# Recurrent block on one core: first gated q^T of a sequence one slot ahead, results kept in traced order on SP, one token sum on another engine

## The chip, the cores and the metric

The kernel runs on one core of a Trainium2 chip. The metric is device time in microseconds of one execution. The engines are named as in the profile: PE (TensorE) multiplies matrices, DVE (VectorE), ACT (ScalarE) and POOL (GpSimd) work on elements, and SP (SyncE) issues most of the transfers between DRAM and SBUF.

## The reference

Eight sequences of 1024 tokens, 512 values each, in fp32. What is computed, cut to what matters:

```python
xn = layernorm(x)                                   # 8 x 1024 x 512
q, gate = xn @ Wq, softmax(xn @ Wg)                 # D = 128, three gates
for i in range(3):                                  # three decays
    k, v = xn @ Wk[i], xn @ Wv[i]
    w = sigmoid(decay_logits[i]) ** max(t - s - 1, 0) * (t > s)
    blended += gate[i] * (((q k^T) * w) v)
s = blended @ Wo * out_scale
g = silu(ffn(xn))        # ffn: silu(xn Gate^T) * (xn Up^T), then Down^T; INTER = 1376
out = x + s * g          # Gate, Up, Down = lut[idx], a table of 16 values
```

## The kernel before

**Two phases.** `phase_1` (0 to 675 us of the profile) makes normalized and transposed tokens, the recurrent part and the weights of the ffn, and leaves all of them in DRAM. `phase_2` (675 to 2227 us) is the ffn and the output. The change touches `phase_1` alone.

**Phase 1, by sequence.** `tokens` loads x in blocks of 128 tokens (SP, L345), takes statistics (DVE for the first two sequences, ACT for the others; POOL raises the variance to the power -0.5), normalizes (DVE, L379, for sequences 0 and 1; ACT, L381 and L382, for the rest), transposes on PE (`pt`, L391) and copies to SBUF on ACT (L392). Values, keys and queries come from `plain` for sequence 0, and from `nodes` for sequences 1 to 7. `nodes` forms its products after Strassen's manner (a block product in seven smaller ones) and needs four sums of the token blocks: `sums_of_tokens` makes t1 (L473) and t2 (L474) on DVE, t3 (L475) and t4 (L476) on POOL; t2 needs t1, and t4 needs t2. `softmax` makes the gates; they are turned around through DRAM: a write of 4-byte elements (L452) and reads that broadcast them over 128 partitions (L457). `keep_tokens` writes the tokens and their sums to DRAM for phase 2 (L480 to L483).

**The recurrence.** `chunks(b)` goes through the 8 chunks of a sequence from the last to the first. For each: `gated(c)` multiplies the gates into q^T (`ga`, L649, POOL; DVE for the last sequence) and that with a table (`qb`, L653, POOL; not for the first chunk taken); PE forms scores (`psc`, L674), DVE weighs them with the decay (`pr`, L676), PE adds up the state (`pu`, L682) and the result (`po`, L696), ACT copies it out (`bl`, L698), SP writes it (L699). Work on a chunk is cut in three parts by `yield`. `gated` is called one chunk ahead, but the first one of a sequence stands at the head of `chunks`.

**The ffn's weights.** `ffn_weights` is a generator of small steps. For each panel of 128 rows it loads indices from 0 to 15, looks them up (`look_up`, DVE, L200, L203, L207, L224), forms sums (POOL, L253 to L279) and writes the panel to DRAM (SP: `quadd`, `wgud`, `wdd`). Panels live in `wgu` with two buffers.

**Order.** Everything of phase 1 is interleaved by hand. The prologue has 12 slots (`plain`), then follow 8 slots for every sequence b, in which `chunks(b-1)` and `nodes(b)` run side by side. A slot has three parts; each begins with `tick()`, which counts down what `defer(parts, issue)` has put off, and pulls some steps of the generators: `fresh` (tokens), `weights`, `older` (chunks) and `newer` (nodes). `sums_of_tokens(b+1)` is called in the last part of the last slot. `keep_order` pins the order so traced for PE, DVE, ACT and POOL; SP is pinned only until slot 3 of the prologue. From there the framework's scheduler may let one SP transfer pass another.

Of the kernel before, what the change touches and what calls it, by code (L numbers as in the profile page):

```python
# [20 lines left out]


ENGINES = (mybir.EngineType.PE, mybir.EngineType.DVE, mybir.EngineType.Activation, mybir.EngineType.Pool)


def keep_order(tc, seen, engines=ENGINES):
# [11 lines left out]
def recurrent_block(ctx: ExitStack, tc, x, wq, wk, wv, wo, wg, decay_logits, out_scale, lut, gidx, uidx, didx, out):  # L38
# [73 lines left out]


    later = []

    def defer(parts, issue):
        later.append([parts, issue])
# [111 lines left out]
    def ffn_weights(build, pool, pair_pool):  # L229
# [9 lines left out]
        def gate_up(o):  # L239
            s, m = OCH[o]  # L240
            n = 2 * NV * m
            idx = build.tile([P, NB], I32, name="idx", tag="idx", bufs=2)
            iv = idx[:, :n].rearrange("p (a b) -> p a b", b=m)
            gs, us = (src[:, s : s + m].rearrange("(c p) b -> p c b", p=P) for src in (gidx, uidx))
            nc.sync.dma_start(out=iv[:, 2:6, :], in_=gs)
            nc.sync.dma_start(out=iv[:, 0:2, :], in_=us[:, 0:2, :])
            nc.sync.dma_start(out=iv[:, 6:8, :], in_=us[:, 2:4, :])
            yield
            wf = pool.tile([P, 2 * NB], F32, name="wgu", tag="wgu", bufs=2)
            yield from look_up(build, wf[:, :n], idx[:, :n], P, n)  # L250
            w = wf[:, : 2 * n].rearrange("p (k two m) -> p k two m", two=2, m=m)
            a21, a11, a12, a22, s1, s2, s3, s4 = (w[:, k] for k in range(8))
            nc.gpsimd.tensor_tensor(s1, a21, a22, ALU.add)  # L253
            nc.gpsimd.tensor_tensor(s2, s1, a11, ALU.subtract)
            yield
            nc.gpsimd.tensor_tensor(s3, a11, a21, ALU.subtract)
            nc.gpsimd.tensor_tensor(s4, a12, s2, ALU.subtract)
            wide = wf[:, 2 * m : 2 * n].rearrange("p (a b) -> p a b", b=m)
            if o >= 4 * NQ:
                defer(3, lambda: nc.sync.dma_start(out=wgu_d[o], in_=wide))  # L260
            if o >= 2 * NK:
                return
            to = quad_d[o // 4][:, :, o // 2 % 2, :].rearrange("p k (t m) -> p k t m", m=P)
            if o % 2 == 0:
                upper.append(w[:, 1:])
                defer(3, lambda: nc.sync.dma_start(out=to[:, :, 0:2, :], in_=w[:, 1:]))
                return
            up, low = upper.pop(), w[:, 1:]
            b21, b22, b11, b12 = low[:, :, 0], low[:, :, 1], up[:, :, 0], up[:, :, 1]
            pair = pair_pool.tile([P, 7, P], F32, name="pair", tag="pair")  # L270
            nc.gpsimd.tensor_tensor(pair, b11, b21, ALU.subtract)
            if o >= 4 * NQ:
                for _ in range(6):
                    yield
            nc.gpsimd.tensor_tensor(b21, b21, b22, ALU.add)
            yield
            nc.gpsimd.tensor_tensor(b11, b21, b11, ALU.subtract)
            yield
            nc.gpsimd.tensor_tensor(b12, b12, b11, ALU.subtract)  # L279
            defer(2, lambda: nc.sync.dma_start(out=to[:, :, 4:6, :], in_=up))  # L280
            defer(3, lambda: nc.sync.dma_start(out=to[:, :, 2:4, :], in_=low))
            defer(3, lambda: nc.sync.dma_start(out=to[:, :, 6, :], in_=pair))
            for _ in range(3):
                yield

        def down_tail():
            s, m = OCH[-1]
            idx = build.tile([P, NB], I32, name="idx", tag="idx", bufs=2)
            nc.sync.dma_start(out=idx[:m, :V], in_=didx[s : s + m, :])
            yield  # L290
            wf = pool.tile([P, 2 * NB], F32, name="wgu", tag="wgu", bufs=2)
            yield from look_up(build, wf[:m, :V], idx[:m, :V], m, V)
            defer(2, lambda: nc.sync.dma_start(out=wdt_d, in_=wf[:m, :V]))

        def down(j):
            idx = build.tile([P, NB], I32, name="idx", tag="idx", bufs=2)
            for a in range(2):
                nc.sync.dma_start(out=idx[:, ts(a, V)], in_=didx[ts(j + a * NK, P), :])
            yield
            t = pool.tile([P, 2 * NB], F32, name="wgu", tag="wgu", bufs=2)  # L300
            yield from look_up(build, t[:, : 2 * V], idx, P, 2 * V)
            b11, b12, b21, b22, t1, t2, t4 = (t[:, ts(k, V // 2)] for k in range(7))
            nc.gpsimd.tensor_tensor(t1, b12, b11, ALU.subtract)
            nc.gpsimd.tensor_tensor(t2, b22, t1, ALU.subtract)
            yield
            nc.gpsimd.tensor_tensor(b12, b22, b12, ALU.subtract)
            nc.gpsimd.tensor_tensor(t4, b21, t2, ALU.subtract)
            defer(3, lambda: nc.sync.dma_start(out=wd_d[j], in_=t[:, : 7 * V // 2]))

        jobs = [gate_up(o) for o in range(NO)] + [down_tail()] + [down(j) for j in range(NK)]  # L310
        next(jobs[0])
# [19 lines left out]
    xnTs = {}  # L331

    def tokens(xp, xnp):

# [37 lines left out]
        def normalize(s):  # L374
            if s >= B * NC:
                return
            xt, (m, r, h) = xts[s], scalars(s)
            if s < 2 * NC:
                nc.vector.tensor_scalar(xt, xt, m, r, ALU.add, ALU.mult)  # L379
            else:  # L380
                nc.scalar.mul(h, m, r)  # L381
                nc.scalar.activation(xt, xt, AF.Identity, bias=h, scale=r)  # L382
# [51 lines left out]
    def softmax(att, b, v_sb, gates, hf, n, waits):  # L434
# [14 lines left out]

        def write():  # L450
            with nc.allow_non_contiguous_dma(reason="1536 words or 3072"):
                nc.sync.dma_start(out=there.rearrange("k p -> p k"), in_=g.rearrange("p c i -> p (c i)"))  # L452

        def read(half):
            m = NC // NHALF * NI
            gates[half] = att.tile([P, m, P], F32, name=f"ga{b}_{half}", tag="ga")
            nc.sync.dma_start(out=gates[half], in_=gT_d[b][ts(half, m), :].partition_broadcast(P))  # L457

        defer(2, write)
        for half, parts in waits:  # L460
            defer(parts, lambda half=half: read(half))

# [5 lines left out]
    def sums_of_tokens(tp, b):  # L468
# [3 lines left out]
        t1, t2, t3, t4 = (ts_[:, k] for k in range(4))  # L472
        nc.vector.tensor_tensor(t1, b12, b11, ALU.subtract)  # L473
        nc.vector.tensor_tensor(t2, b22, t1, ALU.subtract)  # L474
        nc.gpsimd.tensor_tensor(t3, b22, b12, ALU.subtract)  # L475
        nc.gpsimd.tensor_tensor(t4, b21, t2, ALU.subtract)  # L476

    def keep_tokens(b):
        xnT, ts_ = xnTs[b], tss[b]
        nc.sync.dma_start(out=xs_d[b][:, 0:4, :], in_=xnT[:, :, :U])  # L480
        nc.sync.dma_start(out=xs_d[b][:, 4:6, :], in_=xnT[:, 2:4, U:])
        for k in (0, 2):
            nc.sync.dma_start(  # L483
                out=xs_d[b][:, 6 + 2 * k : 10 + 2 * k, :], in_=ts_[:, k : k + 2].rearrange("p a b u -> p (a b) u")
            )

    def plain(sides, att, kept):
# [25 lines left out]
        for k in range(NC + NC // 2):  # L513
            half = iter(())
            if k == NC // 2:
                values(NC - k)
                half = softmax(att, 0, v_sb, gates, 1, NC // NHALF, [(1, 6)])
            if NC // 2 <= k < NC:
                features(1, k - NC // 2, next_role())
            if k >= NC:  # L520

                features(0, k - NC, ("pa", "pe", "pb", "pc")[k - NC])
            if k == NC:
                half = softmax(att, 0, v_sb, gates, 0, NC // NHALF, [(0, 6)])
            next(half, None)
            yield
            next(half, None)
# [107 lines left out]

    def chunks(b, pools, kept):

        chk, blp = pools
        v_sb, gates, qT, kT = kept.pop(b)
        pu = p_r.tile([P, NI, P], F32, name=f"pu{b}", tag="r")  # L640
# [13 lines left out]
            return qa, qb  # L654

        following = gated(NC - 1)
        for c in reversed(range(NC)):
            last = c == NC - 1
            first = c == 0
# [36 lines left out]
                nc.tensor.matmul(po, lhsT=lh, rhs=rh, start=(n == 0), stop=(n == len(prods) - 1))  # L696
            bl = blp.tile([P, P], F32, name=f"bl{b}_{c}", tag="bl")
            nc.scalar.copy(bl, po)  # L698
            defer(1, lambda bl=bl, c=c: nc.sync.dma_start(out=bl_d[b][:, ts(c, P)], in_=bl))  # L699
            if not first:  # L700
                new = chk.tile([P, NI, P], F32, name=f"R{b}_{c}", tag="R")
                if last or not at_end:
# [11 lines left out]
    def phase_1():  # L714
        nonlocal small, p_a, p_c, p_r
        with (
# [8 lines left out]
            tc.tile_pool(name="wgup", bufs=1) as wgup,  # L725
            tc.tile_pool(name="att", bufs=2) as att,
            tc.tile_pool(name="chk", bufs=2) as chk,
            tc.tile_pool(name="blp", bufs=2) as blp,
            tc.tile_pool(name="pairp", bufs=1) as pairp,
            tc.tile_pool(name="small", bufs=3) as small,  # L730
        ):
# [22 lines left out]
            sums = sums_of_weights(sides)  # L754
            for k in range(NC + NC // 2):

                two = k == NC - 1 or k > NC
                tick()
                some(fresh, 3)
                next(setup, None)  # L760
# [3 lines left out]
                next(more, None)  # L764
                tick()
                next(first)
                some(weights, k >= NC // 2)
                some(fresh, 3 * two)
                some(weights, 2 * (k >= NC // 2))
                tick()  # L770
                next(first)
                if k == NC:
                    keep_tokens(0)
                if k >= NC:
                    next(sums)
                if k == 3:
                    keep_order(tc, seen, (mybir.EngineType.SP,))
            sums_of_tokens(tp, 1)
            for b in range(1, B + 1):
                older = chunks(b - 1, (chk, blp), kept)  # L780
                newer = nodes(b, sides, att, kept) if b < B else iter(())
                for k in range(NC):
                    tick()
# [11 lines left out]
                    tick()  # L795
                    next(fresh, None)
                    next(older, None)
                    if k == NC - 1 and b + 1 < B:
                        sums_of_tokens(tp, b + 1)
                    some(weights, 2 * (b < B))  # L800
                    some(newer, 1 - k % 2)
                for g in (older, newer):
                    for _ in g:
# [2 lines left out]
                pass  # L806
            while later:
                tick()

# [482 lines left out]
```

## Time and profile before

| | us |
|---|---|
| median of 3 runs (2225.44, 2225.83, 2227.60) | 2225.83 |
| the profiled execution | 2228.99 |
| its span | 2227.2 |
| phase 1 in it, to the first work of phase 2 | 675 |
| PE busy, DVE, ACT, POOL | 2135.3, 1196.0, 868.7, 1088.1 |
| mean granted clock of PE | 0.982 |

Busy times are sums over an engine's instructions within the span. The granted clock is the share of full speed that PE was allowed. Of a wait the profile names the engine that waited, and after an arrow what released it. Boundaries between sequences, taken as the end of the last product of `nodes` (`pcq`, L621) ahead of `sums_of_tokens`, lie at 98.85 (the end of the prologue), 167.75, 249.72, 331.40, 414.90, 489.98 and 565.70 us.

### The profile page before, as it was taken

To read this page: it belongs to the slowest core of one execution; us is meant where nothing else is said; L and a number is where in the kernel's file an instruction comes from. 1 tells how busy PE (TensorE), PEld (TensorE's weight loads), DVE (VectorE), ACT (ScalarE), POOL (GpSimd) and SP (SyncE) were. 2 spreads that over 40 slices of the span, in tenths; PEclk is the share of its full clock that TensorE was granted. 3 is DMA by queue.
4 is the path that set the end of the run, shared out by engine and by line. 5 is a ranking of instruction groups with operands and counts; after the bars stand their busy time and mean duration, and the time that the engine had idled before them with its cause. 6 is when DMAs were issued, how large, how long until landed. Compare 5 with 4: busy or idle time off the path is not lost.

```text
span 2227.2 us, 27197 instructions
## 1 busy us (share of the span) xinstructions
PE 2135.3 (96%) x9766; PEld 1698.1 (76%) x9766; DVE 1196.0 (54%) x1690; ACT 868.7 (39%) x1901; POOL 1088.1 (49%) x975
## 2 busy tenths in 40 slices
PE   9598897999889999999999999999999999999998
PEld 5477666768766878877887887788788778778877
DVE  7688686668862543543454355345335434534543
ACT  2376565667333422431441243144124314413520
POOL 2767646646433535455453454545344554634442
PEclk9799998999999999999999999999999999999999
DMA  7664454652354433442443344244334424434421
GB/s 185 185 149 150 153 158 154 187 165 73 125 195 160 161 120 123 156 161 87 147 147 116 130 157 159 83 151 147 115 136 151 151 97 152 143 113 144 151 72 52
DMA packets 158460, 309.55 MB, mean 139 GB/s; under 512 B 51731, under 2 KB 94230, under 8 KB 156278
## 3 DMA queue, kind: packets, MB, share of 16 engines
q1 hardware_dynamic: 148486, 283.16, 40.0%
q0 software_dynamic: 7728, 23.86, 2.9%
q8 instruction: 77, 1.26, 0.3%
q10 hardware_dynamic: 2112, 0.79, 0.1%
q14 instruction: 57, 0.47, 0.1%
HBM read 233.98 MB, written 73.80 MB: 138 GB/s over the span
## 4 chain that ended last, share of the span: by engine, by line
PE 88%; POOL 4%; DVE 4%; DMA 2%; issue 1%; ACT 1%; SPq 0%; POOLq 0%; DVEq 0%; ACTq 0%
PE s L918 31%; PE ds L1157 22%; PE sE L918 5%; PE fs L868 4%; PE po L696 3%; PE ds L1168 2%; PE ps L1179 2%; PE pcq L621 2%; PE paq L621 2%; PE peq L621 2%; PE psc L674 2%; PE fsE L868 2%; PE pu L682 1%; PE pev L600 1%; DVE leaf L207 1%
## 5 line engine op out<-in xcount | busy, mean ns | idle before, releaser
L918 PE MATMUL s<-xs,wq 128*128 128x256 f32 x3192 | 715.1, 379 | 0.0
L918 PEld LDWEIGHTS s<-xs,wq 128*128 128x128 f32 x3192 | 605.7, 190 | 94.0 <-issue 7.4
L1157 PE MATMUL ds<-wd,s 128*128 128x256 f32 x1280 | 286.7, 379 | 0.0
L1157 PEld LDWEIGHTS ds<-wd,s 128*128 128x128 f32 x1280 | 243.2, 190 | 33.1
L1157 PE MATMUL ds<-wd,h 128*128 128x256 f32 x960 | 222.9, 379 | 0.0
L1157 PEld LDWEIGHTS ds<-wd,h 128*128 128x128 f32 x960 | 182.3, 190 | 52.5 <-issue 27.1
L1012 POOL TENSOR_TENSOR u<-u,e 128x512 f32<-128x512 f32 x64 | 79.9, 1271 | 276.0 <-DVE u L1008 276.0
L941 DVE TENSOR_TENSOR s<-s,e 128x512 f32<-128x512 f32 x133 | 93.0, 700 | 202.8 <-ACT s L940 202.8
L1182 POOL TENSOR_TENSOR gx<-gx 128x512 f32<-128x512 f32 x63 | 80.3, 1274 | 184.3 <-DVE gx L1180 183.6
L945 DVE TENSOR_TENSOR sE<-s,e 128x512 f32<-128x512 f32 x133 | 93.0, 699 | 102.5 <-PE s L918 102.5
L918 PE MATMUL sE<-xs,wq 128*128 128x256 f32 x532 | 136.5, 379 | 0.0
L936 ACT COPY e<-sE 128x512 f32<-128x512 f32 x133 | 77.9, 586 | 136.5 <-PE sE L918 136.3
L852 POOL TENSOR_TENSOR xs<-xs 128x1792 f32<-128x1792 f32 (+1 forms) x38 | 127.8, 3382 | 1.0
L1198 ACT ACTIVATE gx<-ds 128x256 f32<-128x256 f32 x32 | 12.3, 385 | 285.9 <-PE ds L1168 285.9
L207 DVE TENSOR_SCALAR leaf<-idx,lut_x,lut_sb 128x1024 int32<-128x1024 int32 (+2 forms) x119 | 113.7, 983 | 0.0
L940 ACT COPY s<-s 128x512 f32<-128x512 f32 x133 | 75.8, 570 | 96.8 <-PE s L918 96.8
L929 ACT COPY s<-s 128x512 f32<-128x512 f32 x133 | 75.8, 570 | 95.2 <-PE s L918 92.7
L918 PEld LDWEIGHTS sE<-xs,wq 128*128 128x128 f32 x532 | 101.1, 190 | 13.7
L1190 DVE TENSOR_TENSOR pw<-ds,pw 128x256 f32<-128x256 f32 x32 | 13.6, 425 | 177.0 <-PE ds L1157 177.0
L1016 POOL TENSOR_TENSOR h<-h,e 128x512 f32<-128x512 f32 x64 | 80.0, 1274 | 57.5 <-issue 46.4
L674 PE MATMUL psc<-ga,kT 128*128 128x128 f32 x384 | 58.8, 293 | 51.0 <-POOL ga L649 50.6
L674 PEld LDWEIGHTS psc<-ga,kT 128*128 128x128 f32 x384 | 54.8, 204 | 67.6 <-POOL ga L649 53.9
(220 smaller groups left out, 3799.3 us busy)
## 6 DMA issues: line engine op xcount, KB each, us to landing
wq<-quadd SPq DMA_DIRECT2D x112, 896.0 KB, 4.5
xs<-xsd SPq DMA_DIRECT2D x8, 3584.0 KB, 11.8
wq<-quadd SPq DMA_DIRECT2D x42, 448.0 KB, 4.0
x<-in_x SPq DMA_DIRECT2D x64, 256.0 KB, 4.9
xsd<-ts SPq DMA_DIRECT2D x16, 1024.0 KB, 4.1
gx<-in_x SPq DMA_DIRECT2D x64, 256.0 KB, 2.8
out<-gx POOLq DMA_DIRECT2D x63, 256.0 KB, 2.3
quadd<-wgu SPq DMA_DIRECT2D x15, 896.0 KB, 4.7
```

The source lines that it names most:

```text
L207: nc.vector.tensor_scalar(o.bitcast(I32), iv, lut_x[:rows, k, :], lut_i[:rows, k, 0:1], ALU.bitwise_and, ALU.bitwise_xor,)
L621: nc.tensor.matmul(ps, lhsT=wq_k[k][:, v, ts(n, D)], rhs=xk[k][:, v, :], start=start and v == 0, stop=False, skip_group_check=True,)
L674: nc.tensor.matmul(psc[:, i, :], lhsT=kc[:, i, :], rhs=qa[:, i, :], start=True, stop=True)
L852: nc.gpsimd.tensor_tensor(o, x1, x2, ALU.subtract)
L868: nc.tensor.matmul(ps, lhsT=w[:, 2 * W_OF[k] + n, :m], rhs=xs[:, X_OF[k], 2 * n : 2 * n + 2, :], start=start and n == 0, stop=stop and n == 1,
L918: nc.tensor.matmul(self.t[n][:, ts(a, H)], lhsT=self.w[:, a, (0, 1, 5, 3, 2, 4, 6)[i - 1], :], rhs=self.xs[:, X_OF[self.ks[a]], D_OF[i], : ...
L941: nc.vector.tensor_tensor(self.t[1], self.t[1], self.e, ALU.add)
L945: nc.vector.tensor_tensor(self.t[3], self.t[2], self.e, ALU.add)
L1012: nc.gpsimd.tensor_tensor(o[:, n], o[:, n], other[:, n], ALU.add)
L1016: nc.gpsimd.tensor_tensor(of_h(half, n), of_h(half, n), two(other[:, n]), ALU.mult)
L1157: nc.tensor.matmul(ps, lhsT=lhs[k][:, n, :], rhs=wd_sb[n][:, ts(D_OF[k], H)], start=start and n == 0, stop=stop and n == NK - 1, skip_grou ...
L1182: (nc.vector if end else nc.gpsimd).tensor_tensor(g, g, xr, ALU.add)
```

## The change

- The first `gated` of a sequence is issued one slot ahead: `chunks` yields right after it, and `phase_1` makes and starts `chunks(b)` in the last slot of the sequence before, ahead of `sums_of_tokens(b + 1)`.
- t3 goes from POOL to DVE.
- Transfers of results (weights, gates, tokens, `bl`) and the reads of the gates are issued by `put`, and `keep_behind` gives each of them an order behind the SP instruction traced ahead of it. Transfers that are no results (x, indices) stay free.
- Sequence 1's tokens: ACT normalizes them (`s < NC` where it was `s < 2 * NC`), and the prologue takes double steps of `fresh` at slots 5, 7, 9 and 11, where they were at 7, 9, 10 and 11.
- The write of the gates is put off by 1 part (was 2); sequence 0's reads by 8 and 10 (were 6 and 6).
- The write of `bl` is put off by 2 parts (was 1), and `bl` has four buffers (were two).
- The last four slots of the prologue take no weight steps beyond the first pull of each slot (three fewer for each), and each later slot takes seven (was six). After an odd panel `ffn_weights` yields eight times (was three).
- `keep_tokens(0)` is split over slots 8 and 9.

The diff, cut to its lines:

```diff
 ENGINES = (mybir.EngineType.PE, mybir.EngineType.DVE, mybir.EngineType.Activation, mybir.EngineType.Pool)
+def keep_behind(tc, seen, names):
+    last = None
+    order = mybir.DependencyInfo(mybir.DependencyClass.NoSync, mybir.DependencyReason.DATA)
+    for i in tc.nc.cur_bb.bb.instructions:
+        if i.name not in seen and i.engine == mybir.EngineType.SP:
+            if last and i.name in names:
+                tc.add_manual_dep(i, last, order, reason="behind what was traced before")
+            last = i.name
...
     later = []
+    behind = set()
+    def put(out, in_):
+        nc.sync.dma_start(out=out, in_=in_)
+        behind.add(nc.cur_bb.bb.instructions[-1].name)
...
             if o >= 4 * NQ:
-                defer(3, lambda: nc.sync.dma_start(out=wgu_d[o], in_=wide))
+                defer(3, lambda: put(out=wgu_d[o], in_=wide))
             if o >= 2 * NK:
                 upper.append(w[:, 1:])
-                defer(3, lambda: nc.sync.dma_start(out=to[:, :, 0:2, :], in_=w[:, 1:]))
+                defer(3, lambda: put(out=to[:, :, 0:2, :], in_=w[:, 1:]))
                 return
...
             nc.gpsimd.tensor_tensor(b12, b12, b11, ALU.subtract)
-            defer(2, lambda: nc.sync.dma_start(out=to[:, :, 4:6, :], in_=up))
-            defer(3, lambda: nc.sync.dma_start(out=to[:, :, 2:4, :], in_=low))
-            defer(3, lambda: nc.sync.dma_start(out=to[:, :, 6, :], in_=pair))
-            for _ in range(3):
+            defer(2, lambda: put(out=to[:, :, 4:6, :], in_=up))
+            defer(3, lambda: put(out=to[:, :, 2:4, :], in_=low))
+            defer(3, lambda: put(out=to[:, :, 6, :], in_=pair))
+            for _ in range(8):
                 yield
...
             yield from look_up(build, wf[:m, :V], idx[:m, :V], m, V)
-            defer(2, lambda: nc.sync.dma_start(out=wdt_d, in_=wf[:m, :V]))
+            defer(2, lambda: put(out=wdt_d, in_=wf[:m, :V]))
...
             nc.gpsimd.tensor_tensor(t4, b21, t2, ALU.subtract)
-            defer(3, lambda: nc.sync.dma_start(out=wd_d[j], in_=t[:, : 7 * V // 2]))
+            defer(3, lambda: put(out=wd_d[j], in_=t[:, : 7 * V // 2]))
...
             xt, (m, r, h) = xts[s], scalars(s)
-            if s < 2 * NC:
+            if s < NC:
                 nc.vector.tensor_scalar(xt, xt, m, r, ALU.add, ALU.mult)
...
             with nc.allow_non_contiguous_dma(reason="1536 words or 3072"):
-                nc.sync.dma_start(out=there.rearrange("k p -> p k"), in_=g.rearrange("p c i -> p (c i)"))
+                put(out=there.rearrange("k p -> p k"), in_=g.rearrange("p c i -> p (c i)"))
             gates[half] = att.tile([P, m, P], F32, name=f"ga{b}_{half}", tag="ga")
-            nc.sync.dma_start(out=gates[half], in_=gT_d[b][ts(half, m), :].partition_broadcast(P))
-
-        defer(2, write)
+            put(out=gates[half], in_=gT_d[b][ts(half, m), :].partition_broadcast(P))
+        defer(1, write)
         for half, parts in waits:
...
         nc.vector.tensor_tensor(t2, b22, t1, ALU.subtract)
-        nc.gpsimd.tensor_tensor(t3, b22, b12, ALU.subtract)
+        nc.vector.tensor_tensor(t3, b22, b12, ALU.subtract)
         nc.gpsimd.tensor_tensor(t4, b21, t2, ALU.subtract)
-    def keep_tokens(b):
+    def keep_tokens(b, parts=(0, 1)):
         xnT, ts_ = xnTs[b], tss[b]
-        nc.sync.dma_start(out=xs_d[b][:, 0:4, :], in_=xnT[:, :, :U])
-        nc.sync.dma_start(out=xs_d[b][:, 4:6, :], in_=xnT[:, 2:4, U:])
-        for k in (0, 2):
-            nc.sync.dma_start(
+        if 0 in parts:
+            put(out=xs_d[b][:, 0:4, :], in_=xnT[:, :, :U])
+            put(out=xs_d[b][:, 4:6, :], in_=xnT[:, 2:4, U:])
+        for k in (0, 2) if 1 in parts else ():
+            put(
                 out=xs_d[b][:, 6 + 2 * k : 10 + 2 * k, :], in_=ts_[:, k : k + 2].rearrange("p a b u -> p (a b) u")
...
                 values(NC - k)
-                half = softmax(att, 0, v_sb, gates, 1, NC // NHALF, [(1, 6)])
+                half = softmax(att, 0, v_sb, gates, 1, NC // NHALF, [(1, 8)])
             if NC // 2 <= k < NC:
             if k == NC:
-                half = softmax(att, 0, v_sb, gates, 0, NC // NHALF, [(0, 6)])
+                half = softmax(att, 0, v_sb, gates, 0, NC // NHALF, [(0, 10)])
             next(half, None)
...
         following = gated(NC - 1)
+        yield
         for c in reversed(range(NC)):
...
             nc.scalar.copy(bl, po)
-            defer(1, lambda bl=bl, c=c: nc.sync.dma_start(out=bl_d[b][:, ts(c, P)], in_=bl))
+            defer(2, lambda bl=bl, c=c: put(out=bl_d[b][:, ts(c, P)], in_=bl))
             if not first:
...
             tc.tile_pool(name="chk", bufs=2) as chk,
-            tc.tile_pool(name="blp", bufs=2) as blp,
+            tc.tile_pool(name="blp", bufs=4) as blp,
             tc.tile_pool(name="pairp", bufs=1) as pairp,
...
-                two = k == NC - 1 or k > NC
+                two = k in (NC - 3, NC - 1, NC + 1, NC + 3)
                 tick()
...
                 next(first)
-                some(weights, k >= NC // 2)
+                some(weights, NC // 2 <= k < NC)
                 some(fresh, 3 * two)
-                some(weights, 2 * (k >= NC // 2))
+                some(weights, 2 * (NC // 2 <= k < NC))
                 tick()
                 next(first)
-                if k == NC:
-                    keep_tokens(0)
+                if k in (NC, NC + 1):
+                    keep_tokens(0, (k - NC,))
                 if k >= NC:
                     keep_order(tc, seen, (mybir.EngineType.SP,))
+            following = chunks(0, (chk, blp), kept)
+            next(following)
             sums_of_tokens(tp, 1)
             for b in range(1, B + 1):
-                older = chunks(b - 1, (chk, blp), kept)
+                older = following
                 newer = nodes(b, sides, att, kept) if b < B else iter(())
...
                     next(older, None)
+                    if k == NC - 1 and b < B:
+                        following = chunks(b, (chk, blp), kept)
+                        next(following)
                     if k == NC - 1 and b + 1 < B:
                         sums_of_tokens(tp, b + 1)
-                    some(weights, 2 * (b < B))
+                    some(weights, 3 * (b < B))
                     some(newer, 1 - k % 2)
...
                 tick()
+            keep_behind(tc, seen, behind)
```

## The prediction

> **What bounds the kernel now.** I read the page first, then the windows, then PE's waits, then the timeline at the largest wait. The page's slices:
>
> ```profile
> PE   9598897999889999999999999999999999999998
> ...
> PEclk9799998999999999999999999999999999999999
> ```
>
> A slice is 55.7 us. From slice 13 on PE is full at full clock; before that it dips, and the clock with it. The windows (window, us, then busy of PE, PEld, DVE, ACT, POOL, then the clock, DMA share, GB/s):
>
> ```profile
> 167.75:249.72 81.97, 71.78 (x404) 56.57 (x404) 64.55 (x64) 51.57 (x136) 49.47 (x45) 0.96 0.49 147
> 489.98:565.70 75.72, 70.32 (x404) 56.24 (x403) 66.64 (x69) 48.52 (x128) 42.99 (x37) 0.98 0.39 128
> 174.50:181.00 6.50, 3.53 (x13) 3.53 (x14) 6.43 (x4) 0.00 (x0) 6.42 (x4) 0.50 0.58 242
> 675.00:2227.00 1552.00, 1546.44 (x6564) 1240.02 (x6564) 691.85 (x1073) 504.32 (x946) 711.62 (x629) 1.00 0.39 132
> ```
>
> Phase 2 (from 675) is PE without holes, and the change leaves it alone; its 1552 us stay. All that can be won is in the first 675 us, where PE's idle gaps add to 85.6 us. The first two windows are single sequences of that phase; PE needs 69 to 70 of their 76 to 82 us. The third is the time just after a boundary: clock 0.50. Who held PE in the first 680 us (us in total, times, longest):
>
> ```profile
> PE psc L674 <- POOL ga L649: 50.6, 9, 12.5
> PE pt L391 <- DVE x L379: 16.2, 3, 7.5
> PE pu L682 <- ACT ks L668: 5.5, 1, 5.5
> PE pt L391 <- ACT x L382: 2.9, 1, 2.9
> ```
>
> The first line is the change of sequence: the first score product waits for the first gated q^T. Around the boundary at 167.75, POOL, then DVE, then PE (start, us, engine, line, idle before):
>
> ```profile
> 167.83 2.36 POOL L475 TENSOR_TENSOR ts<-xnT 128x1024 f32<-128x1024 f32 x1 [2.85 <-PE pcq L621]
> 172.61 2.84 POOL L476 TENSOR_TENSOR ts<-xnT,ts 128x1024 f32<-128x1024 f32 x1 [2.42 <-DVE ts L474]
> 175.41 3.99 POOL L649 TENSOR_TENSOR ga<-ga,qT 128x384 f32<-128x384 f32 x2
> ```
>
> ```profile
> 167.84 3.43 DVE L473 TENSOR_TENSOR ts<-xnT 128x1024 f32<-128x1024 f32 x1 [0.43 <-issue]
> 171.31 1.23 DVE L474 TENSOR_TENSOR ts<-xnT,ts 128x1024 f32<-128x1024 f32 x1
> 172.45 0.81 DVE L207 TENSOR_SCALAR leaf<-idx,lut_x,lut_sb 128x1024 int32<-128x1024 int32 x1
> 173.29 5.28 DVE L224 COPY_PREDICATED leaf<-bit,leaf 128x1024 f32<-128x1024 uint8 x2
> ```
>
> ```profile
> 177.47 1.65 PE L674 MATMUL psc<-ga,kT 128*128 128x128 f32 x6 [6.04 <-POOL ga L649]
> ```
>
> POOL does t3 (L475), waits for t2 (L474), does t4 (L476), and only then gates (L649). DVE's list matters too: behind it pr comes at 180.46, and po at 183.36.
>
> **What the Trainium skill says.** (1) "SBUF — State Buffer", section "Who interferes with whom": VectorE and GpSimd share a port pair; a VectorE instruction with two SBUF inputs or in a two-port mode and a reading GpSimd instruction exclude each other for a whole instruction. The trace agrees: L473 takes 3.43 beside L475, 1.22 alone; two L224 take 5.28 across t4 and the gates, 1.30 each alone. (2) "TensorE: Matmul & The Clock Gate", "What's actually happening": an idle window of about 3.4 us halves the clock, and as much activity restores it. The trace agrees: after a stall of 4.52 us the records show 0.50 for 3.4 us; after one of 1.79 none. (3) "DMA: Bandwidth & Descriptors", "Queues, rings and completion order": SP's transfers share a ring on each DMA engine and are consumed in its order. The trace agrees (SP): the g write of 4-byte elements, issued at 62.42, holds the gates' read until 76.73, and x, issued right behind it, first serves at 77.41.
>
> ```profile
> 62.42 0.60 SPq L452 DMA_DIRECT2D gTd<-g  x1
> 63.11 4.73 SPq L345 DMA_DIRECT2D x<-in_x  x3
> 76.73 0.33 SPq L457 DMA_DIRECT2D ga<-gTd  x1
> ```
>
> **The change, part by part.**
>
> (a) *First gate a slot ahead, t3 to DVE.* Removed at six boundaries: PE's stalls of 6.04, 6.95, 12.52, 4.52, 5.35 and 6.62 us = 42.0, and the half-clocked work after them (1.85, 1.4, 2.2, 1.7, 1.6, 2.7, half the busy time in the 0.50 records) = 11.45; together **53.4**. The gate (L649, 1.0 us) now runs before the boundary, when its gates and q^T are long there; POOL idles for 0.4 of a stage (49.5 of 82, 43 of 75.7 busy), so it costs nothing; if POOL were late, it would be late by that 1.0. The t3 that POOL loses (2.36) is counted at DVE below, at 1.22.
>
> *What is late next.* From the boundary PE has work of its own: the next psc comes 3.7 us and po 7.6 us after it, if nothing waits. po needs pr, and pr stands on DVE behind t1, t2, t3 (3 x 1.22 = 3.66) and the table look-ups traced there, and all of them take turns with POOL's t4 (2.34) and the next gates (L649, L653, 1.0 each). The order traced for the changed kernel puts between t1 and pr, at the six boundaries: 3 L207 + 2 L224 (5.0 at 0.80 and 1.30); 4 L207 + 1 L224 (4.5); 2 L224 (2.6); nothing; 4 L207 + 1 L224 (4.5); 5 of L200/L203/L207 (3.56). Lower end, no exclusion: 3.66 + list + 0.55 - 7.6 = 1.6, 1.1, 0, 0, 1.1, 0.2. Upper end, all of t4 and both gates in the way (+4.34): 5.95, 5.45, 3.55, 0.95, 5.45, 4.5 = 25.9. I take the upper less one gate, since the boundary above shows DVE held through all of t4 and part of the gates: 4.95, 4.45, 2.55, 0, 4.45, 3.5 = 19.9, and four of them long enough for half clock, 4 x 1.7 = 6.8. New stalls: **26.7** (4 to 34).
>
> (b) *Seven look-up pulls in each slot instead of six; none in the prologue's last four slots.* Twelve pulls move out of the prologue into the stages. DVE's own work by stage (counts by median durations, t3 included) goes from 52.6, 50.5, 49.2, 42.4, 56.4 and 73.8 to 56.7, 56.2, 53.0, 45.0, 65.9 and 65.3. In the stage 489.98 to 565.70 it showed 66.64 busy for 56.4 of work, a factor of 1.18 from the exclusion; 65.9 gives 78, 8 over PE's 70. POOL gets lighter there, some lag can drain into the next, lighter stage: I take 6, and 1 each for the two stages with 56 (67 against 70, small lags): **8** (0 to 14).
>
> (c) *bl buffers 2 to 4, bl writes a part later.* The last sequence's stall at 650 (5.55) came from the bl copy waiting 7.84 us for its buffer's write, which lay behind a 3.5 MB load:
>
> ```profile
> 655.20 0.27 ACT L698 COPY bl<-po 128x128 f32<-128x128 f32 x1 [7.84 <-DMA bld<-bl]
> ```
>
> Four buffers reach over two more copies, some 7 us (copies at 639, 643, 646): **gain 5.55 + 1.65 of half clock = 7.2** (0 to 7.2).
>
> (d) *Sequence 1's tokens.* Its normalize goes to ACT (two instructions for one, 16 more, in slices where the page shows ACT busy 0.2 to 0.5) and the double steps come at slots 5, 7, 9, 11. The waits at 54.6 (7.48), 63.2, 73.7 and 85.5 sum to 19.1, with 7.95 of half clock; 7.35 more before psc at 91.5. In their place, I judge, come one stall of 6 to 7 us on a scale computed by POOL behind other sums, and one near 81 to 84, where a later x lies behind the g write (13.7 to 17 us each in the trace) and two 1 MB token writes: first scores at 88.5 instead of 98.85, **gain 10.5** (4 to 20).
>
> (e) *Results kept behind on SP; softmax write a part earlier, reads later; keep_tokens in two halves; eight yields after an odd panel.* These change which transfer is ahead of which; SP issues 537 either way. Behind a held write on SP stand x loads (DVE's and ACT's statistics wait), gates' reads and weight writes (their buffers feed DVE's look-ups). I cost them at **zero**, between the two ends named below: the reads moved to 8 and 10 parts (three parts to a slot, 98.85 / 12 = 8.2 us) give the g write over 20 us. If that cover is gone, see the third rival; a gain from fewer collisions is no more than the g write's hold of 14 to 17 us at one place, and lies in (d).
>
> Sum: 53.4 - 26.7 - 8 + 7.2 + 10.5 = 36.4. The profiled execution took 2229.0 (span 2227.2), 3.2 above the median 2225.8; I subtract from the median: **2189 us**.
>
> **Rivals.**
> 1. *The wait only moves to DVE* (0.24). Upper ends throughout: stalls 25.9, half clock at five places 8.5, lag 12; boundaries net 7, bl 7, prologue 4: 18, so 2208. For it: the 5.28 us of L224 before pr at 180.46. Against it: POOL has one operation fewer to take turns with.
> 2. *All clears* (0.16): look-ups slip past pr without harm, prologue at its upper end: 53.4 + 7.2 + 20 = 81, so 2145. Against it: the list between t1 and pr.
> 3. *SP's order holds the weights* (0.11), the side on which it is slower: a panel's quad write, kept behind a g write of 14 to 17 us, keeps one of two wgu buffers; DVE's L207 for the next panel stands still, and behind it pr, so PE. Five odd panels at 12 us are 60: 2249. It decides from 8 us a panel (40 > 36). For it: SP waited 126.8 us on that write in nine times; against it: DVE's one wait of this kind was 2.62 us, and a panel lasts a slot and more longer now.
>
> **How the numbers follow.** Forecast 0.49, with its own range 2175 to 2203. The range 2143 to 2216 takes in rivals 1 and 2 and leaves out rival 3 and the tails. A measurement of this kernel tells about 0.2%, 4.5 us, from no change. Slower: 0.11, rival 3. Within: 0.06, the bad end of rival 1. Faster: the rest, 0.83.
>
> **What would show it.** Right: psc's waits for POOL near zero at the six boundaries; po waiting for pr on DVE, 2 to 5 us, in their place, none at the fifth; the boundary stages 70 to 77 us; no wait near 650; first scores at 84 to 93; phase 2 still 1552. Wrong: psc still waiting on ga; L207 waiting for quadd writes; a stage above 82 us.

## The result, and the profile after

The changed kernel takes 2198.3 us (median; 2197.66 to 2199.03) against 2225.9, a ratio of 0.9875 (95% interval 0.9858 to 0.9892). Forecast were 2189 us (2175 to 2203), a gain of 36; measured is a gain of 27.6. The profiled execution took 2199.0 (span 2197.2), 30.0 below that of before. The page's slices, PE and its clock:

```profile
PE   9789889999899999999999999999999999999998
...
PEclk9899999999999999999999999999999999999999
```

The dips are still in phase 1, which now ends at 648.56 instead of 678.58 (start of the first `fs`). The windows (us, then busy of PE, PEld, DVE, ACT, POOL, clock, DMA share, GB/s) show two boundary stages and phase 2, whose 1548.6 us are those of before:

```profile
153.36:231.86 78.50, 71.74 (x403) 57.06 (x403) 64.31 (x67) 51.60 (x135) 50.36 (x44) 0.96 0.61 168
...
461.50:541.31 79.81, 72.73 (x403) 56.95 (x403) 73.73 (x77) 48.90 (x127) 42.96 (x38) 0.96 0.46 126
648.56:2197.20 1548.64, 1542.90 (x6557) 1238.38 (x6555) 692.32 (x1073) 504.34 (x946) 708.50 (x628) 1.00 0.39 132
```

In the second line DVE is busy for 73.7 of 79.8 us; in the same stage of before it was 66.6 of 75.7. PE's waits in phase 1 (us, times, longest):

```profile
PE po L718 <- DVE pr L698: 21.2, 5, 5.8
PE psc L696 <- POOL ga L670: 12.9, 6, 5.6
PE pt L409 <- ACT x L400: 11.7, 3, 5.0
PE pbq L640 <- ACT pbq L590: 6.8, 5, 2.6
PE pcv L619 <- DVE v L603: 4.8, 5, 1.9
```

The wait of 50.6 us for `ga` has become 12.9, and po's wait for `pr` has grown from 1.3 to 21.2. Its line in the kernel before:

```profile
PE po L696 <- DVE pr L676: 1.3, 2, 0.9
```

(L698, L696, L670, L718 are the old L676, L674, L649, L696; `look_up`'s L207 and L224 are now L224 and L241.) DVE behind the first boundary:

```profile
154.71 1.23 DVE L492 TENSOR_TENSOR ts<-xnT,ts 128x1024 f32<-128x1024 f32 x1
155.86 1.22 DVE L493 TENSOR_TENSOR ts<-xnT 128x1024 f32<-128x1024 f32 x1
156.99 2.86 DVE L224 TENSOR_SCALAR leaf<-idx,lut_x,lut_sb 128x1024 int32<-128x1024 int32 x1
159.88 1.97 DVE L241 COPY_PREDICATED wgu<-bit,leaf 128x1024 f32<-128x1024 uint8 x1
161.76 2.20 DVE L224 TENSOR_SCALAR leaf<-idx,lut_x,lut_sb 128x1024 int32<-128x1024 int32 x2
163.99 1.30 DVE L241 COPY_PREDICATED leaf<-bit,leaf 128x1024 f32<-128x1024 uint8 x1
165.18 0.55 DVE L698 TENSOR_TENSOR pr<-psc,w_tab 128x384 f32<-128x384 f32 x1
```

PE formed the scores at 156.88, and pr comes 8 us later: five look-up instructions stand between, and the first takes 2.86 for its 0.80, for it takes turns with POOL's t4 (156.07 to 159.30). So po starts only at 165.78, after 4.76 us of idleness.

Phase 1 of the two profiled executions, cut at the first scores and at each boundary:

| stretch, us | before | after | gain | forecast |
|---|---|---|---|---|
| prologue, to the first scores | 98.85 | 84.02 | 14.8 | 10.5 |
| stage 1 (no boundary stall in either) | 68.89 | 69.34 | -0.5 | 0 |
| six boundary stages | 473.6 | 465.8 | 7.7 | 18.7 |
| last sequence | 37.27 | 29.38 | 7.9 | 7.2 |

The gains add up to 30.0 and not to 27.6, since the profiled execution of before ran 3.1 us above its median, and that of the changed kernel 0.6. Within the six stages, PE's idle time fell from 50.6 to 40.8 us, and what half clock cost (half of the busy time under a 0.50 record, a stretch that the profile marks with that clock) rose from 11.5 to 12.5. A second profile of the changed kernel has 82.8, 71.5, 464.1 and 29.4 in the table's order, and 9.9 for half clock; so a stretch is known to about 2 us, and half clock to nearly 3.

### The profile page after: what moved, and what is told of

It is laid out like the page before. It is cut to its first block, busy times and chain, and to the rows that moved or that the text cites. A ratio compares the mean times of both kernels' runs of the same rounds, so it can differ in the third digit from the quotient of the medians.

```text
span 2197.2 us, 27201 instructions
## 1 busy us (share of the span) xinstructions
PE 2132.1 (97%) x9766; PEld 1694.0 (77%) x9766; DVE 1190.5 (54%) x1690; ACT 878.2 (40%) x1917; POOL 1074.4 (49%) x967
## 4 chain that ended last, share of the span: by engine, by line
PE 85%; DVE 8%; POOL 2%; DMA 2%; issue 2%; ACT 0%; POOLq 0%; DVEq 0%
PE s L946 31%; PE ds L1185 22%; PE sE L946 5%; PE fs L896 4%; PE ds L1196 2%; PE ps L1207 2%; DVE leaf L224 2%; PE po L718 2%; PE pcq L640 2%; PE peq L640 2%; PE paq L640 2%; PE fsE L896 2%; DVE leaf L241 1%; DVE wgu L241 1%; DMA x<-in_x 1%
## 5 line engine op out<-in xcount | busy, mean ns | idle before, releaser
L224 DVE TENSOR_SCALAR leaf<-idx,lut_x,lut_sb 128x1024 int32<-128x1024 int32 (+2 forms) x119 | 113.9, 985 | 0.0
L674 POOL TENSOR_TENSOR qb<-ga,q_tab 128x384 f32<-128x384 f32 x56 | 73.3, 1309 | 55.8 <-DVE ga L670 29.5
L1222 POOL TENSOR_TENSOR pw<-pw 128x256 f32<-128x256 f32 x32 | 34.7, 1084 | 134.4 <-DVE pw L1221 134.4
```

The source lines that it names most:

```text
L224: nc.vector.tensor_scalar(o.bitcast(I32), iv, lut_x[:rows, k, :], lut_i[:rows, k, 0:1], ALU.bitwise_and, ALU.bitwise_xor,)
```

## The experiments

Each kernel was timed beside the kernel before. That one's median lies between 2225.9 and 2230.3 us from chip to chip, so ratios to it are compared: 0.9875 (0.9858 to 0.9892) is the changed kernel's. "Six stages" is the sum of the boundary stages in the profile: 465.8 and 464.1 in two profiles of the changed kernel, and 464.0 in a run that leaves these stages alone. "First scores" is the end of the prologue: 81.9 to 86.1 us over six profiles of kernels with the changed kernel's prologue.

Theory 1, with which I began: the look-ups that are traced between t1 and the first pr make the wait, at that place. Its rival: DVE is too full around there, and the wait shows wherever the look-ups are put.

**The look-ups put off until after pr.**

```diff
-                    some(weights, 2)                     # first part of a slot
+                    some(weights, 2 * (k > 0) + (0 < k < 6))
-                    some(weights, 3 * (b < B))           # last part
+                    some(weights, 3 * (b < B and k < NC - 1))
```

> The changed kernel, with the five look-up pulls between the token sums and the first pr of a sequence (three in the last part of slot 7, two in the first part of slot 0) moved to the first parts of slots 1 to 5; the same work. Theory 1 (the traced list of look-ups between t1 and pr holds po): po's waits for DVE fall from 21.2 us to 5 or less, the half-clocked loss of the six stages from 12.5 to 5 or less, total about 2180 (2172 to 2188). Rival (DVE is full over a whole stage, so the stall comes back at another place): 2194 to 2202.

Ratio 0.9870 (0.9857 to 0.9884): no difference from the changed kernel, the rival's side. PE's waits:

```profile
PE pcv L619 <- DVE v L603: 21.0, 8, 4.7
...
PE psc L696 <- POOL ga L670: 12.1, 5, 4.3
```

The wait for pr (21.2 us) is gone entirely, and the wait for another DVE result (`v`, L603) has grown from 4.8 to 21.0, by 16.2. Over phase 1 PE is idle for 3.7 us less (59.4 to 55.7), and half clock costs 5.0 more (17.3 to 22.3). The list does hold pr, but most of what is put off comes back in the next slots: theory 1's saving falls.

**One part alone: the first gate a slot ahead.** The kernel before, with only the `yield` and the lines on `following` from the diff.

> The kernel before with one part of the change alone: the first gate a slot ahead; t3 stays on POOL. Theory 1: psc's waits for POOL at the boundaries go from 42 us to under 10, po's waits for DVE of about 20 take their place, total 2208 (2202 to 2214). Rival (the gate is worth nothing without t3 leaving POOL, since the second gate then waits behind t3 and t4): 2218 to 2228.

Ratio 0.9947 (0.9935 to 0.9959), -12.4 us: less than I expected, just beyond the rival's end. The first scores come at 93.4 instead of 98.9, but stage 1 grows from 68.9 to 75.0 and takes it back. In the six stages (462.2, against 473.6) po waits 15.9 for DVE, and psc still waits 14.2 for POOL: at the second boundary 8.1 us, for POOL has t3, t4 and a panel's sums ahead of the second gate, and at the third 3.9, for a panel's sums stand even ahead of the first.

**t3 back on POOL.**

```diff
-        nc.vector.tensor_tensor(t3, b22, b12, ALU.subtract)
+        nc.gpsimd.tensor_tensor(t3, b22, b12, ALU.subtract)
```

> The changed kernel with t3 back on POOL. Theory 1 (t3 is 1.2 us in DVE's list, or about as much through the exclusion): 2196 to 2202. Rival (t3's move carries the gain): 2206 or more. Second rival (t3 on DVE is what holds pr): 2190 or less.

Ratio 0.9896 (0.9881 to 0.9911), a loss of 4.6 us by the ratios, though the intervals overlap; six stages 470.8, some 5 to 7 more. The median of 2207.0 lies in the first rival's range, but on this chip the kernel before takes 2230.3, 4.4 more than on the first; by the ratio t3's move is worth a little more than theory 1 gave it, and far from all of the gain. po waits 23.7 instead of 21.2. So taking t3 from DVE does not relieve it: beside POOL's t3, t1's median grows from 1.22 us to 2.38, about what t3 itself takes.

**Without the order on SP's transfers of results.** The call of `keep_behind` left out.

> The changed kernel without the order on SP's transfers of results. Costed at zero in the prediction: 2194 to 2203, with the same waits of PE. Rival (the order carries part of the prologue's gain of 14.8): 2205 to 2214, with the first scores after 88 us instead of 84. Second rival (it costs): 2192 or less.

Ratio 0.9875 (0.9861 to 0.9888), as forecast. The profile has the first scores at 88.2, 2 us beyond the range above, and then the same waits; phase 1 ends 3 us later. The order moves a few us in the prologue at most, within what the times can tell.

**The changed kernel again, on the chip of the next three.**

> The changed kernel itself, to have it beside the three below on one chip. Both theories: 0.9875 of the kernel before (0.986 to 0.989).

Ratio 0.9870 (0.9855 to 0.9885), 2198.2 us.

**Sequence 1's tokens as before.** `s < 2 * NC` and `two = k == NC - 1 or k > NC` put back.

> The changed kernel with sequence 1's tokens as before: DVE normalizes them and the double steps come at slots 7 and 9 to 11. Theory 1 (the prologue's gain of 14.8 us comes from the tokens' order): 8 to 15 us above the changed kernel, the first scores at 93 to 99 instead of 84. Rival (it comes from the look-up pulls that left the prologue, or from the transfers' order): within 4 us of the changed kernel.

2197.4 us, ratio 0.9867 (0.9851 to 0.9884): no difference. The first scores come at 83.8 against 82.8. The prologue's gain is not the tokens' order: the rival is right in that, and what carries the gain instead this run does not show.

**The look-ups' pace as before.** Pulls in the prologue's last four slots, six in each later slot, three yields.

> The changed kernel with the look-ups' pace as before: pulls in the prologue's last four slots, six in each later slot, three yields after an odd panel. Theory 1 (DVE's lumps of look-ups hold PE at the boundaries, and seven pulls make them larger): stages shorter by 5 to 10 us together, prologue longer by 0 to 6, in all 8 us below to 2 above the changed kernel. Rival (the pulls in the prologue were what held PE there, and with three yields DVE waits for buffers being written): 5 to 20 us above.

2200.5 us, ratio 0.9880 (0.9866 to 0.9895): not told from the changed kernel, but two halves cancel. Prologue 89.1 instead of 82.8, six stages 457.2 instead of 464.1, both beyond their spread, and the total 2.4 us above the changed kernel's, just past the end of theory 1's range. So the old pace costs in the prologue about what it saves behind it; which of its three edits does what was not parted.

**Two bl buffers.** `blp` with `bufs=2`.

> The changed kernel with two bl buffers instead of four; the write stays two parts behind. Theory 1 (the buffers are the end of the last sequence's stall): 5 to 9 us above the changed kernel, pu waiting for ACT ks behind a bl copy again. Rival (the stall went by the transfers' order): within 3 us.

2208.3 us, ratio 0.9916 (0.9901 to 0.9931): 10.2 us slower, a little more than the 5 to 9 of theory 1. ACT on the last sequence:

```profile
633.98 0.27 ACT L720 COPY bl<-po 128x128 f32<-128x128 f32 x1 [6.98 <-DMA bld<-bl]
```

The copy waits for its buffer's write, and PE loses 6.9 us there, as forecast. Another 4.8 are lost in stage 5 (391 to 466), where a bl copy waited 6.2 us for the same reason and the scores waited for ACT behind it: a place at which two buffers did no harm before, when the write was issued a part earlier.

By now theory 1 had fallen, and theory 2 stood in its place: all that is left in the stages comes from lumps of look-ups on DVE; its lag holds po and pcv directly, and psc by way of panel sums that POOL starts late.

**Less work on DVE: the look-ups' predicated copies left out.**

```diff
-            nc.vector.copy_predicated(o, bits[level - 1][:rows, :n], t[:rows, :n])
             yield
```

> The changed kernel with the predicated copies of the look-ups left out (seven of a panel's nineteen DVE instructions, 1.30 us each and more beside POOL; the weights come out other than the reference's). Theory 2 (lumps of look-ups on DVE make all that is left of PE's waits in the stages: po, pcv, and by late panel sums psc): six stages of 69 to 72 us instead of 69 to 80, total 2198 - 40 = 2158 (2150 to 2168). Rival (PE is held by the chain from PE over ACT or POOL and back, whatever DVE does): 2185 or more.

2164.9 us, ratio 0.9711 (0.9698 to 0.9724), six stages 436.1:

```profile
PE po L717 <- DVE pr L697: 13.0, 4, 5.1
PE pt L408 <- ACT x L399: 7.8, 3, 4.3
PE psc L695 <- POOL ga L669: 6.7, 3, 4.6
```

The waits of pcv and pbq are gone, po's fall by 8.2 us and psc's by 6.2, and the total lies in theory 2's range. Seven of nineteen instructions take PE's idle time in the six stages from 40.8 to 17.9 us: DVE's look-ups are shown to make more than half of it. Not parted is how. POOL, with the same instructions, is busy for 327.2 us of phase 1 instead of 365.9, so a share may come through the turns that the two engines take and not through the length of DVE's list.

**The later gates a part earlier.** POOL at the largest wait for a gate (the gate is the last line; PE waited 5.62 us for it):

```profile
321.13 0.72 POOL L270 TENSOR_TENSOR wgu<-wgu 128x256 f32<-128x256 f32 x1 [2.58 <-DVE wgu L241]
...
328.42 2.07 POOL L294 TENSOR_TENSOR wgu<-wgu 128x896 f32<-128x896 f32 x1
330.45 0.99 POOL L670 TENSOR_TENSOR ga<-ga,qT 128x384 f32<-128x384 f32 x1
```

A panel's sums stand ahead of it, and they began late, for they waited 2.58 us for DVE's last look-up.

```diff
-            yield
             if not first:
                 following = gated(c - 1)
+            yield
```

> The changed kernel with every later gate of a sequence called one part earlier, so ahead of the steps of weights pulled in that part. Theory 2 (psc's waits of 12.8 us come from panel sums of 10 us that stand ahead of the gate in POOL's order): psc's waits under 4 us, total 8 to 15 us below the changed kernel (2183 to 2190). Rival (POOL's own lag; the gate is late wherever it stands, or DVE's lag takes up what is won): within 4 us of 2198.

Ratio 0.9889 (0.9875 to 0.9902), no gain: six stages 467.8. psc's waits fall from 12.9 to 3.1, as I expected, and the total is the rival's:

```profile
PE pbq L640 <- ACT pbq L590: 8.4, 5, 2.8
PE pcv L619 <- DVE v L603: 7.4, 6, 2.0
PE psc L696 <- POOL ga L670: 3.1, 2, 1.9
```

pcv and pbq take part of it, and at the same place PE now waits 4.6 us for a normalized block: ACT waited 5.25 for its scale from POOL (L390), which stands behind the panel's sums as the gate did. In all, half clock costs 22.6 us over phase 1 instead of 17.3.

**The look-ups taken ahead of the boundary.**

```diff
-                    some(weights, 3 * (b < B))
+                    some(weights, (3 + (3 < k < 7) - 3 * (k == 7)) * (b < B))
```

> The changed kernel with the three look-up pulls of slot 7's last part taken in slots 4, 5 and 6, ahead of the boundary instead of behind it. Theory 2 (what counts is how full DVE is over a whole slot, and slots 4 to 6 have room): po's waits fall by 10 us or more and no others rise by half of that; 6 to 16 us below the changed kernel. Rival (as with the pulls put off to slots 1 to 5: the same microseconds show at another wait): within 4 us.

2187.1 us, ratio 0.9811 (0.9797 to 0.9824), 13 to 14 us below the changed kernel by the ratios, and the intervals are apart: theory 2. It beats both kernels.

```profile
PE psc L696 <- POOL ga L670: 13.7, 6, 5.1
PE pcv L619 <- DVE v L603: 10.4, 6, 2.6
PE po L718 <- DVE pr L698: 6.8, 4, 2.2
```

po's waits fall by 14.4, and pcv's rise by 5.6. In the six stages (451.8 instead of 465.8) PE's idle time shrinks by 9.3 us (40.8 to 31.6) and the loss under half clock by 5.5 (12.5 to 7.0; by 2.9 against the second profile's 9.9). One long wait has often become two short ones, and of those fewer cost the clock: PE's stage gaps of over 4 us fall from five to one.

**The same, with an evener pace.** Last parts pull two in slots 0 to 2, three in slots 3 to 6, none in slot 7; three yields.

> The version of look-ups taken early, with a slower and evener pace besides: last parts pull two in slots 0 to 2, three in slots 3 to 6, none in slot 7; three yields after an odd panel, as before. The same work. Theory 2 (DVE's fullness in the slots behind a boundary holds PE): pcv's and psc's waits of 24 us fall by 5 or more, 2180 to 2186. Rival (with three yields the look-ups wait for panels still being written, 11.3 us in the kernel before): 2188 to 2197.

2187.2 us, ratio 0.9810 (0.9797 to 0.9824): the same, between the ranges of theory 2 and its rival. pcv's and psc's waits fall from 24.1 to 17.4, but DVE's look-ups wait 11.0 us for panels that are still being written (1.9 in the changed kernel), and stages 3 and 4 are longer by 1.5 and 2.7 us: theory 2 and its rival both have their part.

## Why the prediction was right or wrong

**(a) The removed boundary stalls: right.** No first psc of a sequence waits for POOL at the six boundaries any more; the scores there come on time.

**The new wait for pr: right in kind and size.** Step by step 4.95, 4.45, 2.55, 0, 4.45, 3.5 was forecast; 4.76, 4.90, 1.55, 0, 4.17, 5.81 was measured, 21.2 for 19.9. Taking the upper end less one gate was a judgment, and it held but for the last, which lies above the upper end of 4.5. There POOL did two panel sums (L323 and L324, 1.17 us each) between t4 and the gate, and DVE's three L217 beside them took 5.11 us; the count of what DVE takes turns with had left these sums out:

```profile
547.90 1.17 POOL L323 TENSOR_TENSOR wgu<-wgu 128x256 f32<-128x256 f32 x1
545.64 5.11 DVE L217 TENSOR_SCALAR bit<-idx 128x1024 uint8<-128x1024 uint8 x3
```

**The half clock behind the new stalls: mis-sized.** Four stalls at 1.7 each, 6.8, came out as 12.5, from five stages with 1.5 to 3.3 us each. I had counted po's stalls alone, and one record of 3.4 us for each. Three of the records last 6.8 us, and psc's 5.62 us at 325.88 and a wait of pbq of 2.65 at 506 each brought another. In the second profile that last one is missing and the loss is 9.9, so the term is short by 3 to 6 us.

**(b) DVE short over a stage: right in direction, too small.** Forecast were 8 us. PE's other idle time in the six stages rose from 8.6 (50.6 less the 42.0 of the boundaries) to 19.6, by 11.0. The forecast named DVE's lag, but not where it would come out: in the gates behind panel sums (psc 9.6), in pbq (6.8) and in pcv (2.9). The twelve pulls that leave the prologue were costed in the stages alone, and their gain in the prologue (6.3 with the rest of the pace) was not put down to them.

These two terms, 5.7 and 3 us, and po's 1.3 are most of the missing 11 in the six stages (1 more is PE's work itself). The prologue came out 4 us better than forecast, and not for the reason given in (d). That was luck, and it brought the total nearer than its parts were.

**(c) bl: right.** 7.9 us for 7.2, and the buffers are its cause; their worth in the changed kernel, with its later write, is more, 10.2, since stage 5 needs them too.

**(d) Sequence 1's tokens: the step that failed.** The 10.5 us were worked out from the tokens' schedule (98.85 less 88.5 is 10.35), but with the old token order the gain stays. Two stalls of 5.0 came in the prologue, at 54.87 and 74.17. The second is the one named for 81 to 84: ACT waited 1.99 us for an x, which landed earlier than forecast. The first is not the one named. POOL's last scale before it was done at 51.84; ACT stood in the softmax's exponential (L460) and waited for DVE, which came late to it from a copy of the look-ups beside POOL's t4:

```profile
53.75 3.43 DVE L241 COPY_PREDICATED wgu<-bit,leaf 128x1024 f32<-128x1024 uint8 x1
57.26 0.78 DVE L459 TENSOR_TENSOR g<-v,red 128x12 f32<-128x12 f32 x1
58.07 0.21 ACT L460 ACTIVATE g<-g 128x12 f32<-128x12 f32 x1 [6.44 <-DVE g L459]
```

What carried the gain in its place is shown in part. psc's wait before the first scores, 7.35 us in the kernel before, is 1.5 now and 2.8 with the gate alone moved ahead; that run's first scores gained 5.5, which stage 1 took back. PE's waits for x, 19.1 us before, are 11.7 now, 13.0 with the old token order and 17.6 with the look-ups' old pace, which costs 6.3 in the prologue; the order on SP is worth perhaps 4. These don't simply add, each is known to 2 us or worse, and how the 14.8 divide between them and the softmax's new delays wasn't settled.

**(e) Transfers at zero: held, as far as tried.** SP's waits for the g write fell from 126.8 us to 64.8 in phase 1; without the order on SP they are 110.3, and the time is the same. The softmax's write and reads and the halves of `keep_tokens` were not tried alone.

**The rivals.** The first was partly what happened: the wait moved to DVE, and the stage's lag was nearer its 12 than my 8. The third did not come: look-ups waited 1.9 us for panels. Here the prediction had also misread the kernel before: not one wait of 2.62 but three of 11.3 us in all. The five more yields took them away: with three yields they are 12.9 (the look-ups' old pace) and 11.0 (the evener pace).

## What to carry to other kernels

When a wait at one engine is taken away, cost what the next consumer in the same chain stands behind on its own engine; that list, with the turns that the engine takes with another, gave the new waits here to within 7% in sum, and to 1 us at all boundaries but the one where the other engine's work was not fully counted. When an engine is full in lumps, putting its work off past the critical result brings most of the wait back at the next result (16.2 of 21.2 us); taking the work ahead of the boundary, where there was room, shortened it. Splitting a long wait saves the clock too, where that falls after long ones: 3 to 5.5 of the 12 to 14 us in the six stages.

## What the hardware showed beyond expectation

Over the fourteen profiles of this case, take PE's waits after the first scores of phase 1 that began at full clock. A record of 0.50 followed none of 60 waits from 1.2 to 1.75 us, 13 of 35 up to 2.75, 12 of 14 up to 3.25, and all 62 longer ones. Many of these are one wait seen in several profiles, and the ends of matmuls are modelled. At pbq's wait of 2.65 us at 506.24 the record starts at 508.6, while PE still waits. So the bound isn't sharp, and here it lies nearer 2 to 3 us than the 3.4 us of idleness that the Trainium skill ("TensorE: Matmul & The Clock Gate", "What's actually happening") gives and with which I reckoned. The shortest whole record of half clock lasts 3.4 us, in agreement with what the page gives for the way back.
